# A quantised 3x3 convolution and a 7x7 involution: six x buffers instead of five, and narrower band buffers

## The chip, the cores and the metric

The kernel runs on one core of one Trainium2 chip. The metric is the device time of one execution in microseconds (us). Three runs of the kernel before were taken; a profile of one further execution gives every view quoted below.

## The reference, cut to what matters

```python
# x: (32, 256, 32, 32) float32
# layer 0
x = x + quant_conv3x3(group_norm(x), weight, bias)      # 256 -> 256 channels, values rounded to fp16's range and mantissa
# layer 1, an involution: every pixel has its own 7x7 kernel, one for each of 16 groups of channels
g = group_norm(x)
y = relu(bn(w1 @ g))                                    # 256 -> 64 channels
w = w2 @ y + b2                                         # 16 groups * 49 taps, for every pixel
x = x + sum over the 49 taps k of w[group, k, pixel] * g[channel, pixel + offset(k)]
```

`group_norm` has 32 groups of 8 channels; it needs the sums over a whole image before it can scale one element, so that an image passes through the kernel in stages.

## The kernel before, in words

An image is two halves of 128 channels by 1024 pixels, 1 MB of float32. One loop over steps `n` runs everything; an image takes `per` = 16 steps, and each piece of work on image b stands at a fixed distance from step 16 b. The order of the work on every engine is written out by this loop; nothing is rearranged later.

- **Loading x.** `load_x` (line 106) issues two transfers of 512 KB on SyncE's queue (SP), at step 16 b - 63, some four images ahead. The tile comes from the pool `xpool` with 5 buffers (line 94): the tile of image b takes the room of image b - 5.
- **The front** (`front`, from step 16 b - 56) is group norm, the 3x3 convolution on TensorE (line 332, `pc`), the residual addition, the second group norm, `py` (line 377) and the transposition of the normalised pixels (line 396, `pt`).
- **The involution's weights.** `weights` (line 411, eight calls for an image) makes the 49 x 16 weights of four rows of pixels; VectorE moves them into the ring `w_sb` (line 435). `scatter` (line 476, SP's queue) writes them to DRAM (`wd`) in the layout of a band matrix, 7 transfers of 160 KB for each of the 4 blocks k of eight rows of an image.
- **The bands.** `load_bands` (line 497) reads a block back from `wd` into one of three band buffers, by 16 transfers of 40 to 70 KB: 14 on GpSimd's queue (POOL), 2 on SP's (`BY_SYNC`). A band buffer has two sides, left and right half of the rows of pixels, each with `WINC` = 22 columns of `WB` = 160 floats and a pad of 8 floats.
- **The sums.** `sums` (line 522) multiplies bands and pixels on TensorE, two calls for a block (one for each side), eight for an image; of the 22 columns of a side it reads 19 (`WINI`), since three lie outside of the image. `add_windows` (line 538, VectorE) adds the result to x in place.
- **The stores.** `store` (line 543, SP's queue) writes half an image, 512 KB, when its sums are added. The second store of image b - 5 stands two steps before the load of image b, and the load writes the same buffer.

SP's queue is in order. Around the load of x it has, for every image: ... the last scatters, the second store, two band loads (block 2), **the two loads of x**, four scatters (block 0 of the next image), two band loads (block 3), three and four scatters (blocks 0 and 1), two band loads, and so on. In the compiled program the first of the two loads of x waits for the landing of the second store. Also, SP's transfers take eight semaphores in turn, so that each issue waits for the landing of the transfer eight places before it, where it doesn't wait for more. Counted so, the fourth scatter after the loads of x takes the semaphore of that store.

Of the kernel before, what the change touches and what calls it, by code (L numbers as in the profile page):

```python
# [9 lines left out]
F32 = mybir.dt.float32  # L10
# [3 lines left out]
P = 128  # L14
# [6 lines left out]
K1, PAD1 = 7, 3  # L21
# [15 lines left out]
XR = 4  # L37
# [3 lines left out]
SIDES = 2  # L41
JC = W // SIDES
K = H // TR
M = K * SIDES
WIN = XR + K1 - 1
WINC = JC + K1 - 1
WINI = JC + PAD1


# [2 lines left out]
V = 2  # L52
A = G // V
WB = G * WIN
PAD = V * (TR - XR)
WPIX = K1 * WB + PAD
SW = K1 * G
S = H + 2 * PAD1
T = 4
# [2 lines left out]
PAIRS = G // 2  # L62
ROW = S * WPIX
WR = 4
NBAND = 3
# [5 lines left out]
EARLY = CH + 4 + CH * CR  # L71
LATE = K1 * SW + 2 * 2 * SW
FRONT = -56
# [5 lines left out]
def tile_quant_conv_then_involution(  # L79
# [11 lines left out]
    PSUM = bass.MemoryType.PSUM  # L91

    const = ctx.enter_context(tc.tile_pool(name="const", bufs=1))
    xpool = ctx.enter_context(tc.tile_pool(name="xpool", bufs=5))
    small = ctx.enter_context(tc.tile_pool(name="small", bufs=2))
    work = ctx.enter_context(tc.tile_pool(name="work", bufs=2))
    dram = ctx.enter_context(tc.tile_pool(name="dram", bufs=1, space=bass.MemoryType.DRAM))
# [41 lines left out]
        nc.gpsimd.memset(t, 0.0)  # L139

    y_sb = [const.tile([P, N // 2], F32, name=f"y_{i}") for i in range(2)]
    bands = [const.tile([P, SIDES, WINC * WB + PAD], F32, name=f"band_{i}") for i in range(NBAND)]
    for t in bands[CH:]:
        nc.gpsimd.memset(t, 0.0)
    pixels = [const.tile([P, 2, PAIRS, PAIR], F32, name=f"pixels_{i}") for i in range(NPIX)]
# [4 lines left out]
    w_sb = const.tile([P, 2, RING, A, WIN, V], F32, name="w_sb")  # L150
    wd = dram.tile([H, S, WPIX], F32, name="wd")
    acc = [ps_acc.tile([P, RG, NT], F32, name=f"acc_{d}") for d in range(SIDES)]
# [14 lines left out]
    nc.sync.dma_start(late_sb, late)  # L167
    w2_sb = late_sb[:, : K1 * SW].rearrange("p (k n) -> p k n", n=SW)
    b2_sb = late_sb[:, K1 * SW :].rearrange("p (e r n) -> p e r n", r=2, n=SW)

# [10 lines left out]
    for col, cols, at, n in (  # L181
# [4 lines left out]
        to = bass.AP(  # L186
            tensor=wd.tensor,
            offset=wd.offset + col * WPIX + at,
            ap=[[ROW, H], [WPIX, cols], [1, n]],
        )  # L190
# [212 lines left out]
    def weights(b, r0):  # L403

        pws = [ps_w.tile([P, 2, 2, SW], F32, tag=f"pw{i}", name=f"pw{i}") for i in range(2)]
        for r in range(2):
# [58 lines left out]
    def scatter(b, k, part):  # L465

        at = (b * H + k * TR) % RING
        for dj in range(part, K1, 2):
            t, e = divmod(dj, 2)
            to = bass.AP(  # L470
                tensor=wd.tensor,
                offset=wd.offset + k * TR * ROW + dj * WPIX + (K1 - 1 - dj) * WB,
                ap=[[WPIX, TW], [ROW, TR], [1, WB]],
            )
# [3 lines left out]
    def load_bands(b, k):  # L478

        band = bands[(b * K + k) % NBAND]  # L480
        side = WINC * WB + PAD
        for i, j in enumerate(ORDER):
            cut = max(0, PAD1 - j)
            n = (K1 - cut) * WB + PAD
            src = bass.AP(
                tensor=wd.tensor,
                offset=wd.offset + k * TR * ROW + (j + PAD1) * WPIX + cut * WB,
                ap=[[ROW - V, TR], [(W - 1 - 2 * j) * WPIX - cut * WB, SIDES], [1, n]],
            )
            to = band[j::JC]  # L490
            to = bass.AP(
                tensor=to.tensor,
                offset=to.offset + (j + cut) * WB,
                ap=[to.ap[0], [side + (JC - 1 - 2 * j - cut) * WB, SIDES], [1, n]],
            )
            queue = nc.sync if j in BY_SYNC else nc.gpsimd
            queue.dma_start(to, src)  # L497

    def windows(b, m):


        k, d = divmod(m, SIDES)
        for g in range(RG):
            top = k * TR + g * XR - PAD1
            at = acc[d][:, g, : CH * WINI * WIN].rearrange("p (h j r) -> p h j r", h=CH, r=WIN)
            yield g, at, top, max(top, 0), min(top + WIN, H)

    def sums(b, m):

        k, d = divmod(m, SIDES)  # L510
        j0 = 0 if d else PAD1
        band = bands[(b * K + k) % NBAND][:, d]
        px = pixels[(b * K + k) % NPIX][:, d]
        for h in range(CH):
            for v in range(2):
                for g, at, top, f, l in windows(b, m):
                    p = slice(g * KP, (g + 1) * KP)
                    of = band[p, V * g * XR + j0 * WB : V * g * XR + (j0 + WINI) * WB]
                    of = of.rearrange("p (j a r v) -> p j a r v", a=A, r=WIN, v=V)
                    for t in range(T):  # L520
                        a = h * T + t
                        nc.tensor.matmul(  # L522
                            at[t * TW : (t + 1) * TW, h, :, f - top : l - top],
                            px[p, a, v * GC : v * GC + TW],
                            of[:, :, a, f - top : l - top, v],
                            start=(h, v) == (0, 0),
                            stop=(h, v) == (CH - 1, 1),
                        )
# [20 lines left out]
    def due(n, lag):  # L549

        b, i = divmod(n - lag, per)
        return (b, i) if 0 <= b < B else (None, None)

    with tc.manual_schedule():
        fronts = {}
        for n in range(FRONT, B * per + 2):
            b, i = due(n, FRONT)
# [12 lines left out]
            b, i = due(n, 0)  # L570
            if b is not None and i % 2 == 0:
                sums(b, i // 2)
            b, i = due(n, 1)
# [6 lines left out]
            b, i = due(n, 2)  # L580
            if b is not None and i == 2 * (M - 1 - SIDES):
                store(b, 0)
            b, i = due(n, -LEAD)
# [3 lines left out]
            for part in range(2):  # L587
                b, i = due(n, -LEAD + 1 + part)
# [4 lines left out]
            b, i = due(n, LOAD)  # L593
# [3 lines left out]
            b, i = due(n, 3 - 4 * NBAND)  # L597
            if b is not None and i % 4 == 0:
                load_bands(b, i // 4)
# [38 lines left out]
```

## Time and profile before

| | us |
|---|---|
| median of three runs | 1356.12 |
| lowest and highest | 1348.22 and 1360.93 |
| the profiled execution | 1344.24 |
| its span, first to last instruction | 1342.5 |
| TensorE busy in the span | 1253.6 (93%) |
| GpSimd (POOL) busy | 1014.4 (76%) |
| VectorE (DVE) busy | 818.8 (61%) |
| ScalarE (ACT) busy | 733.3 (55%) |

The profile names an instruction by its line, engine, operation and tiles, as `out<-in`. "A <- B" in a list of waits means that A's engine stood idle until B was done. "issue" is idle time for which no awaited event is found. PE is TensorE, SPq the queue of SyncE, where each item is the issue of a transfer. The DMA share in tables of time windows is the mean busy share of the core's 16 DMA engines (where it is over 1, packets overlap).

### The profile page before, as it was taken

How to read it: one execution, taken by the hardware profiler on the slowest of the kernel's cores; microseconds unless marked ns; L12 is line 12 of the kernel's file. 1: busy time of each engine (PE TensorE's matmuls, PEld its weight loads, DVE VectorE, ACT ScalarE, POOL GpSimd, SP SyncE). 2: the span in 40 equal slices, each digit the busy share in tenths (PEclk: the TensorE clock that was granted, in tenths of full speed). 3: DMA queues.
4: the chain of work that ended last, by engine and by line, in shares of the span. 5: the costliest groups of instructions: out<-in, count | busy, mean ns of one | idle time of the engine just before them, and what ended most of it. 6: DMA issues, size and time to landing. Idle time of an engine off the chain costs nothing.

```text
span 1342.5 us, 65799 instructions
## 1 busy us (share of the span) xinstructions
PE 1253.6 (93%) x27648; PEld 763.7 (57%) x27648; DVE 818.8 (61%) x2539; ACT 733.3 (55%) x1731; POOL 1014.4 (76%) x1818
## 2 busy tenths in 40 slices
PE   5899999999999999999999999999999999999665
PEld 2356566565555655556655556666555566556454
DVE  3466666565666665656665666766666666666442
ACT  5775656455656556556545655655556564553300
POOL 9067878777787778777778787788777877788785
PEclk9999999999999999999999999999999999999987
DMA  6089999999999999999999999999999999999995
GB/s 228 11 237 295 271 293 293 279 266 281 272 286 282 291 285 270 283 263 280 293 282 283 270 288 282 293 297 296 281 288 275 277 284 290 271 281 266 278 274 166
DMA packets 360724, 361.85 MB, mean 270 GB/s; under 512 B 75056, under 2 KB 304752, under 8 KB 359152
## 3 DMA queue, kind: packets, MB, share of 16 engines
q1 hardware_dynamic: 278512, 229.38, 56.8%
q0 software_dynamic: 81920, 128.28, 33.9%
q8 instruction: 220, 3.60, 1.1%
q14 instruction: 72, 0.59, 0.1%
HBM read 176.60 MB, written 180.76 MB: 266 GB/s over the span
## 4 chain that ended last, share of the span: by engine, by line
PE 60%; DMA 23%; POOL 7%; issue 3%; ACT 3%; DVE 2%; SPq 1%; POOLq 0%; DVEq 0%; ACTq 0%
PE pc L332 25%; PE acc L522 19%; DMA band<-wd 17%; PE pw L411 11%; POOL band L497 7%; DMA wd<-w_sb 6%; PE pt L396 3%; PE py L377 3%; ACT junk L214 1%; SPq L476 1%; DVE w_sb L435 1%; DMA x<-in_x 1%; ACT xn L273 0%; SPq L497 0%; ACT xq L273 0%
## 5 line engine op out<-in xcount | busy, mean ns | idle before, releaser
L497 POOL DMA_DIRECT2D band<-wd x1792 | 980.3, 549 | 315.7 <-DMA band<-wd 182.0
L435 DVE TENSOR_TENSOR w_sb<-pw,late_sb 128x224 f32<-128x224 f32 (+7 forms) x1280 | 330.4, 322 | 419.5 <-PE pw L411 419.2
L332 PE MATMUL pc<-xq,wq 128*128 128x496 f16 (+3 forms) x2304 | 535.2, 379 | 20.3 <-ACT xq L273 18.3
L522 PE MATMUL acc<-band,pixels 64*32 64x190 f32 (+1 forms) x16384 | 426.6, 332 | 51.8 <-DMA band<-wd 42.7
L522 PEld LDWEIGHTS acc<-band,pixels 64*32 64x32 f32 x16384 | 304.7, 107 | 159.7 <-issue 81.1
L332 PEld LDWEIGHTS <-wq 128*128 128x128 f16 x2304 | 206.7, 98 | 316.1 <-issue 102.7
L411 PE MATMUL pw<-late_sb,y 64*32 64x224 f32 (+1 forms) x8192 | 288.9, 333 | 10.8 <-issue 9.4
L538 DVE TENSOR_TENSOR x<-acc,x 128x380 f32<-128x380 f32 (+1 forms) x512 | 262.0, 512 | 32.2 <-PE acc L522 23.2
L411 PEld LDWEIGHTS pw<-late_sb,y 64*32 64x32 f32 x8192 | 186.5, 106 | 38.1 <-issue 21.0
L400 ACT COPY pixels<-pt 128x512 f32<-128x512 f32 x128 | 73.7, 576 | 228.6 <-PE pt L396 228.6
L214 ACT ACTIVATE junk<-x 128x512 f16<-128x512 f32 (+1 forms) x192 | 146.4, 763 | 14.7 <-DVE x L348 12.2
L214 ACT ACTIVATE junk<-x,mean 128x1024 f16<-128x1024 f32 x128 | 147.1, 1149 | 4.3
L245 ACT ACTIVATE s<-back,eps 128x2 f32<-128x2 f32 x64 | 18.9, 296 | 178.6 <-DVE back L230 178.6
L346 DVE TENSOR_SCALAR q<-pc 128x512 f16<-128x512 f32 x128 | 87.2, 681 | 17.6 <-PE pc L332 17.6
L273 ACT ACTIVATE xn<-x,off,rstd 128x512 f32<-128x512 f32 x128 | 96.2, 800 | 0.0
L348 DVE SCALAR_TENSOR_TENSOR x<-q,early_sb,x 128x512 f32<-128x512 f16 x128 | 94.2, 736 | 0.3
L396 PEld LDWEIGHTS pt<-ident,xn 128*128 128x128 f32 x512 | 63.9, 142 | 26.3 <-issue 2.5
L396 PE MATMUL pt<-ident,xn 128*128 128x128 f32 x512 | 78.0, 275 | 0.1
L273 ACT ACTIVATE xq<-x,off,rstd 128x1024 f16<-128x1024 f32 x64 | 75.7, 1227 | 0.0
L235 ACT ACTIVATE mean<-back 128x2 f32<-128x2 f32 x64 | 12.6, 196 | 101.4 <-DVE back L230 101.4
L377 PE MATMUL py<-xn,early_sb 128*64 128x512 f32 x256 | 62.2, 606 | 0.9 <-ACT xn L273 0.9
L224 DVE STREAM_TRANSPOSE across<-sums 128x32 f32<-128x32 f32 x128 | 26.3, 205 | 33.6 <-ACT junk L214 32.4
(40 smaller groups left out, 369.3 us busy)
## 6 DMA issues: line engine op xcount, KB each, us to landing
wd<-w_sb SPq DMA_DIRECT2D x896, 160.0 KB
band<-wd POOLq DMA_DIRECT2D x1664, 70.5 KB, 4.6
x<-in_x SPq DMA_DIRECT2D x64, 512.0 KB
out<-x SPq DMA_DIRECT2D x64, 512.0 KB
band<-wd POOLq DMA_DIRECT2D x128, 60.5 KB, 4.6
band<-wd SPq DMA_DIRECT2D x128, 50.5 KB
band<-wd SPq DMA_DIRECT2D x128, 40.5 KB
band<-in_w SPq DMA_DIRECT2D x2, 1152.0 KB
```

The lines of the kernel that those rows point to most:

```text
L214: nc.scalar.activation(junk[:, n0:n1], src[:, h, n0:n1], func, bias=bias, accum_out=self.sums[:, i : i + 1])
L273: nc.scalar.activation(dst, src, AF.Identity, bias=self.off[:, one], scale=self.rstd[:, one])
L332: nc.tensor.matmul(pc.rearrange("p (r c) -> p r c", c=W)[:, r0 - nt * RT : r1 - nt * RT, c0:c1], wq[:, kh, k, mh * P : (mh + 1) * P], xq[: ...
L346: nc.vector.tensor_scalar(q, pc, F16_MAX, -F16_MAX, ALU.min, ALU.max)
L348: nc.vector.scalar_tensor_tensor(xt[:, mh, cols], q, bias_sb[:, mh : mh + 1], xt[:, mh, cols], ALU.add, ALU.add)
L377: nc.tensor.matmul(py[i * CR : (i + 1) * CR], w1_sb[:, kh, :], px[:, :, i], start=kh == 0, stop=kh == CH - 1,)
L396: nc.tensor.transpose(pt[:, i, h * P : (h + 1) * P], xn[:, h, (m + i) * P : (m + i + 1) * P], ident)
L411: nc.tensor.matmul(pws[i][t * TW : (t + 1) * TW, : dj.stop - dj.start, r], y_sb[b % 2][half, (r0 // 2 + r) * W : (r0 // 2 + r + 1) * W], w ...
L435: nc.vector.tensor_tensor(to, of[:, :, d0:d1], bias[:, :, d0:d1], ALU.add)
L497: queue.dma_start(to, src)
L522: nc.tensor.matmul(at[t * TW : (t + 1) * TW, h, :, f - top : l - top], px[p, a, v * GC : v * GC + TW], of[:, :, a, f - top : l - top, v], ...
L538: nc.vector.tensor_tensor(x_at, of, x_at, ALU.add)
```

## The change

`xpool` gets six buffers, so that the tile of image b takes the room of image b - 6. To make room, a side of a band buffer keeps only the 19 columns that are inside the image: its length `SIDE` is `WINI * WB + PAD` = 3048 floats in place of 3528. The left side drops its first three columns, the right side its last three; the destination offsets in `load_bands` and the operand's offset in `sums` follow. No transfer and no matmul changes its size or its number. Three memsets of a band buffer cover 6096 elements a partition in place of 7056.

```diff
-WINC = JC + K1 - 1
 WINI = JC + PAD1
...
 WPIX = K1 * WB + PAD
+SIDE = WINI * WB + PAD
...
-    xpool = ctx.enter_context(tc.tile_pool(name="xpool", bufs=5))
+    xpool = ctx.enter_context(tc.tile_pool(name="xpool", bufs=6))
...
-    bands = [const.tile([P, SIDES, WINC * WB + PAD], F32, name=f"band_{i}") for i in range(NBAND)]
+    bands = [const.tile([P, SIDES, SIDE], F32, name=f"band_{i}") for i in range(NBAND)]
...
     def load_bands(b, k):
 
         band = bands[(b * K + k) % NBAND]
-        side = WINC * WB + PAD
...
-                offset=to.offset + (j + cut) * WB,
-                ap=[to.ap[0], [side + (JC - 1 - 2 * j - cut) * WB, SIDES], [1, n]],
+                offset=to.offset + (j + cut - PAD1) * WB,
+                ap=[to.ap[0], [SIDE + (JC - 1 - 2 * j - cut + PAD1) * WB, SIDES], [1, n]],
...
     def sums(b, m):
 
         k, d = divmod(m, SIDES)
-        j0 = 0 if d else PAD1
...
-                    of = band[p, V * g * XR + j0 * WB : V * g * XR + (j0 + WINI) * WB]
+                    of = band[p, V * g * XR : V * g * XR + WINI * WB]
```

In the compiled program every engine's instructions keep their order. The first of the two loads of x, from image 5 on, loses its wait for the store; the fourth scatter behind it gains one for the same store.

## The prediction

> **What bounds the kernel now.** I read the page first, then the time by windows, the waits of TensorE and of the queues, and last the timeline of SP and POOL around one load of x. The page has TensorE busy for 93% of the span and 9 in nearly all slices of its DMA row, so two resources are close to full. The windows say how close. The first two lines are stretches of 200 us in the steady part, the other three are three images with no gap on TensorE at all:
>
> ```profile
> 340.00:540.00 200.00, 194.12 (x4393) 118.66 (x4400) 127.89 (x399) 115.22 (x274) 152.66 (x280) 1.00 0.97 282
> 940.00:1140.00 200.00, 193.86 (x4364) 117.67 (x4348) 126.76 (x395) 114.63 (x273) 153.88 (x283) 1.00 0.97 282
> ...
> 795.06:833.00 37.94, 37.94 (x865) 23.41 (x865) 25.26 (x80) 22.75 (x55) 29.21 (x54) 1.00 0.98 290
> 833.00:871.05 38.05, 38.05 (x865) 23.21 (x864) 25.28 (x80) 22.78 (x55) 29.65 (x55) 1.00 0.97 285
> 871.05:908.99 37.94, 37.94 (x865) 23.17 (x864) 25.26 (x80) 22.75 (x55) 30.49 (x56) 1.00 0.98 295
> ```
>
> The first number is the length, the second TensorE's busy time, the last two the DMA share and GB/s. An image costs TensorE 37.9 to 38.05 us when nothing stops it. The mean period is longer: the 27 loads of x that wait start between 136.2 and 1166.7 us, so 1030.5 / 26 = 39.6 us. So about 1.6 us of each image could go, 43 us over 27 images, before TensorE alone is the bound. The DMA engines stand at 0.96 to 0.98 in both kinds of stretches.
>
> What TensorE lacks, and what the queues wait for:
>
> ```profile
> PE acc L522 <- DMA band<-wd: 29.3, 18, 4.6
> ...
> POOL band L497 <- DMA band<-wd: 153.7, 193, 2.9
> POOL band L497 <- DMA wd<-w_sb: 21.6, 22, 3.1
> ...
> SPq L476 <- DVE w_sb L435: 73.5, 51, 5.1
> SPq L106 <- DMA out<-x: 69.4, 25, 4.1
> SPq L476 <- DMA x<-in_x: 14.4, 18, 1.6
> ```
>
> (total us, times, longest; TensorE's line between 80 and 1300 us, the others between 140 and 1140.) TensorE's largest wait with a named cause is for bands. POOL, which issues most of them, waits for their landings (153.7 us) and for scatters (21.6), hardly ever for a band buffer. So the stream evict, scatter, band load is late, and the DMA engines set its pace. SP stands 69.4 us in front of the loads of x, 2.8 us an image, until the store of the buffer's last owner has landed.
>
> One load of x on SP:
>
> ```profile
> 610.41 0.58 SPq L543 DMA_DIRECT2D out<-x  x1
> 611.09 2.17 SPq L497 DMA_DIRECT2D band<-wd  x2
> 616.29 1.57 SPq L106 DMA_DIRECT2D x<-in_x  x2
> 618.54 2.54 SPq L476 DMA_DIRECT2D wd<-w_sb  x4
> ```
>
> SP is free at 613.26 and issues at 616.29. The DMA engines during such holes (four us each, from 2 us before a load of x to 2 us after):
>
> ```profile
> 614.29:618.29 4.00, 4.00 (x107) 2.74 (x106) 2.71 (x10) 3.11 (x6) 3.66 (x7) 1.00 0.74 179
> 693.04:697.04 4.00, 4.00 (x107) 2.74 (x105) 2.98 (x10) 2.29 (x4) 3.29 (x7) 1.00 0.72 201
> 773.54:777.54 4.00, 4.00 (x103) 2.91 (x106) 3.18 (x11) 2.08 (x4) 3.35 (x7) 1.00 0.79 204
> 851.62:855.62 4.00, 4.00 (x107) 2.74 (x106) 2.65 (x10) 2.74 (x6) 3.26 (x7) 1.00 0.83 213
> 889.85:893.85 4.00, 4.00 (x107) 2.71 (x106) 2.67 (x10) 3.00 (x6) 3.20 (x7) 1.00 0.84 218
> 965.66:969.66 4.00, 2.75 (x73) 2.09 (x78) 2.49 (x9) 2.77 (x6) 2.58 (x6) 1.00 0.89 250
> ```
>
> The reader is to see the share fall to 0.72 to 0.89, and at first without harm: TensorE is full in five of the six.
>
> [...] all SP issues behind the load of x stand still until 616.29. [...] in this image POOL waits 0.93 and 1.14 us for band landings at 621.5 and 623.0, while x drains. [...]
>
> **The change part by part.**
> 1. The wait at line 106 goes: 77.1 us in 27 waits over the whole span, 2.86 us each. SP can issue x at once (613.3 in the image shown). Behind it, three scatters need only evictions and older landings; the evictions of the right `weights` call (TensorE 611.85 to 612.9 us) are done at about 614. The fourth scatter now waits for the store, which landed at about 616.2, and was issued at about 620.2 before. So scatters of block 0 move up by 2 to 4 us, and so do the landings of x that the next scatters wait for (14.4 us, 18 times). None of this is time by itself: SP waits 73.5 us for evictions elsewhere in the steady part, 2.9 us an image, so its lead is taken back there.
> 2. The hole is filled. The mean of the six shares above is 0.80; with 0.89, 0.77 and 0.93 measured for three more loads it is 0.82. Against the 0.965 of the steady part this is 0.143 x 4 us = 0.57 us of all DMA engines for an image; against 1.00, 0.71 us. If the DMA engines set the pace, this comes off the period: 27 x 0.57 = 15.4 us, at most 27 x 0.71 = 19 us. Nothing, if another latency takes over. I take 15.4.
> 3. POOL's waits for scatters (21.6 us in the steady part) lie in about half of the cases 13 to 16 us after a load of x, at block 0 of the next image (1.90 us at 630.88 in the image shown). They shrink. I book no further gain for it: POOL's transfers behind are paced by the engines that item 2 already counts.
> 4. Narrower bands: a memset of 5.97 us covers 6096 in place of 7056 elements, 5.16 us, so 0.81 us less three times. The first frees SP's zero writes 0.8 us sooner; TensorE starts at 15.24 us behind ScalarE, and the first band load stands at 71.7 us. Zero; at most 0.8 us. Matmuls and transfers have the same shapes; their offsets differ, and I take nothing for it.
> 5. The first 136 us and the end after 1167 us have no load of x that waits; the end, where TensorE waits 2 to 4.6 us at a time for bands, stays.
>
> Sum: 1344.24 - 15.4 = 1328.8 us for the profiled execution (span 1342.5 and 1.7 around it). The median of the three runs is 11.9 us above this execution, so I subtract the same from 1356.12: **1340.7 us**, 1.1% faster.
>
> **Rivals.**
> - *The gain is lost (1351 us, 0 to 8 us off).* The hole costs little, because POOL's loads use it: they get more of the engines then. Filled, the hole only moves the slowness from the band loads after it to those within it. For: TensorE is full in five of six holes, and three images in a row ran at 38 us with holes in them. Against: bytes that move earlier can't be in the way later. At 0.2 us an image, 5 us.
> - *Slower (1372 us).* One mechanism: the x load now collides with the POOL loads of block 2, which run just then (608.78 to 618.45 us in the image shown). Block 2's last landing, 617.90 plus the median 4.6 us, is 622.5, and TensorE wants it at 624.72, so there are 2.2 us to spare. From first to last issue blocks that meet x now (block 3) take 9.9 us in the mean, block 0, without x, 8.0; if these 1.9 us move to block 2 and no lead is won, the slack is gone in half of the images, at some 1.2 us each: 27 x 0.6 = 16 us. It decides once block 2 slips by over 2.2 us. Against: the POOL stream as a whole gets no more work.
> - *More (1321 us).* SP's lead of 2 to 4 us keeps scatters ahead in all blocks, and most images reach 38.3 us: 27 x 1.3 = 35 us. Against: the waits for evictions in item 1.
> - *It doesn't do what it says:* the load could be stopped by another semaphore. Its own two semaphores belong to scatters eight places back, which have landed by then in the image shown; 3% within "lost".
>
> **How the numbers follow.** Chances: forecast 0.43 (8 to 21 us off), lost 0.30, slower 0.12, more 0.15. A measurement of this kernel tells about 1%, 13.6 us, from no change. Over 1% faster: all of "more" and 0.30 of the forecast, 0.45; within 1%: the rest of the forecast, "lost", and part of the slower case's weak form (0.02 of it), so 0.45; slower by over 1%: 0.10. The range reaches to "more" and to a half-sized slower case: 1322 to 1364.
>
> **What would show it.** Right: no SP wait for `out<-x` at the load of x; a DMA share around it of 0.95 or more; period of the loads 39.0 us; POOL's waits for scatters below 12 us; TensorE's waits for bands fewer. Wrong: the share stays at 0.8 (another wait took its place); or share filled and period still 39.6 (lost); or TensorE waiting at block 2, 7 to 12 us after x, in most images (slower).

## The result, and the profile after

The changed kernel takes 1366.85 us (median of 13 runs, 1360.91 to 1375.31); the kernel before takes 1354.56 us in 13 runs beside it. The ratio is 1.0103, with a 95% interval of 1.0072 to 1.0134: slower by 1.0%, where 1.1% faster was forecast; the range given ended at 1364 us. The profiled execution has a span of 1370.5 us. Executions of either kernel differ by some 10 us to both sides; a second profile of the changed kernel (below, "again") has a span of 1346.3 us and the same pattern of waits. So the ratios of many runs carry the verdicts here, and of the profiles only what returns in several. Runs more than 1.5% above their kernel's fastest are left out of the ratios (one of narrow5's and one of rev1k's below are among them).

Item 1 of the prediction's working came true, and item 2's first half too. In the changed kernel's file `load_bands` is line 496, `sums` 520 and `store` 541. First windows of the steady part, then the stretches around and behind one load of x (length, TensorE busy, other engines, granted clock, DMA share, GB/s):

```profile
140.00:1140.00 1000.00, 952.82 (x21282) 578.81 (x21279) 625.88 (x1954) 564.80 (x1340) 755.98 (x1382) 1.00 0.96 277
340.00:540.00 200.00, 190.26 (x4294) 116.02 (x4276) 124.36 (x387) 113.19 (x269) 151.67 (x278) 1.00 0.96 275
940.00:1140.00 200.00, 190.12 (x4222) 114.53 (x4219) 125.67 (x394) 112.74 (x269) 149.85 (x274) 1.00 0.96 277
```

```profile
576.60:580.60 4.00, 4.00 (x89) 2.50 (x69) 2.16 (x9) 0.77 (x3) 3.73 (x8) 1.00 1.11 320
580.60:590.60 10.00, 7.80 (x208) 5.16 (x208) 4.87 (x15) 4.57 (x11) 5.45 (x11) 1.00 0.95 279
590.60:600.60 10.00, 9.83 (x216) 6.10 (x215) 6.58 (x18) 7.52 (x18) 7.31 (x14) 1.00 0.92 261
```

The second fence follows one load of x at 578.60 us. The hole is gone: 1.11 in the four microseconds in which the kernel before had 0.72 to 0.89. Over the 26 loads between 140 and 1190 us the mean is 1.04 (309 GB/s), where the kernel before has 0.85 (236 GB/s). But in the ten microseconds behind this load TensorE loses 2.2 us, and in the next ten the share is 0.92. The hole was not removed, it moved. These are the means of GB/s over the images between 140 and 1150 us, counted from the issue of the second store, some 3 us before the changed kernel's load and 6 us before the old one's:

| | 4 to 8 us | 16 to 20 us | 24 to 28 us |
|---|---|---|---|
| before | 236 | 274 | 249 |
| after | 270 | 225 | 229 |
| again | 270 | 242 | 231 |

The share over the whole steady part doesn't tell the kernels apart: it is 0.97 before and 0.96 after, but 0.97 in again and 0.96 in narrow5 and pause6, two kernels below that keep the time of the kernel before.

The queue's timeline around this load, and SP's waits between 140 and 1140 us:

```profile
575.26 0.98 SPq L541 DMA_DIRECT2D out<-x  x1
576.34 2.16 SPq L496 DMA_DIRECT2D band<-wd  x2
578.60 1.00 SPq L106 DMA_DIRECT2D x<-in_x  x2
579.96 3.54 SPq L476 DMA_DIRECT2D wd<-w_sb  x4
583.61 1.86 SPq L496 DMA_DIRECT2D band<-wd  x2
586.94 7.07 SPq L476 DMA_DIRECT2D wd<-w_sb  x7
```

```profile
SPq L476 <- DVE w_sb L435: 146.2, 76, 8.3
SPq L476 <- DMA x<-in_x: 59.9, 43, 3.7
SPq L476 <- DMA wd<-w_sb: 23.2, 34, 2.0
```

The load goes out 0.1 us after the band loads, and no wait for `out<-x` is left in front of it. Its 69.4 us have gone to two other places in the same queue: scatters wait 45.5 us more for the landing of x (59.9 for 14.4), since they now reach the shared semaphores early, and 72.7 us more for evictions (146.2 for 73.5; in again 62.6 and 129.1). SP gained no lead that anybody could use.

Where TensorE's time went: its waits between 80 and 1200 us in the changed kernel (total us, times, longest),

```profile
PE pw L411 <- issue: 17.9, 14, 3.4
PE acc L520 <- issue: 12.9, 13, 2.4
PE acc L520 <- DMA band<-wd: 7.4, 8, 1.9
PE acc L520 <- DMA x<-in_x: 4.2, 3, 2.4
PE pc L332 <- issue: 4.2, 2, 3.9
...
PE pt L396 <- issue: 0.9, 1, 0.9
```

and in the kernel before:

```profile
PE acc L522 <- DMA band<-wd: 14.9, 12, 2.7
PE pw L411 <- issue: 8.5, 14, 1.1
PE acc L522 <- issue: 3.6, 5, 1.2
...
PE pc L332 <- issue: 0.4, 1, 0.4
```

The waits for bands halve, as the prediction wished (14.9 to 7.4). The waits called "issue", for which the profile has no awaited event, grow from 12.5 to 35.9 us. This is nearly all that the two executions differ by: from the 1,501st to the 24,301st of TensorE's matmuls the changed kernel takes 1073.2 us and the kernel before 1048.5, 24.7 of the 28.0 us between their spans, and the issue waits are 23.4 us of it. One of them, in TensorE's timeline 10 us after the load of x:

```profile
584.82 0.60 PE L396 MATMUL pt<-ident,xn 128*128 128x128 f32 x4
585.35 0.88 PE L520 MATMUL acc<-band,pixels 64*32 64x190 f32 x23
588.43 1.07 PE L520 MATMUL acc<-band,pixels 64*32 64x190 f32 x36 [2.20 <-issue]
```

TensorE stops in the middle of the 64 matmuls of one call of `sums`, and the profile has no semaphore there that it waits for. What goes with such stops stands in the DMA part of the page:

```profile
q8 instruction: 220, 3.60, 1.1%
```

These are 220 packets of 16 KB in the queue "instruction". The trace has 56,456 instructions of TensorE (55,296 matmuls and weight loads, and 1,160 others), 256.6 for a packet; 220 x 256 is 56,320. Two things tie the packets to the "issue" stalls of TensorE over 0.5 us after 80 us, of which the changed kernel has 22 and the kernel before 14. First, in all 36 the last such packet had ended 1.2 to 1.7 us before TensorE went on. Second, counted through all of TensorE's instructions in the trace, all 36 stalls stand at the same two neighbouring places of a period of 256. Over the 17 profiles of this document the first holds for 271 of 277 stalls and the second for 272; a place that had nothing to do with the period would fall on these two once in 128. So I read these stalls as TensorE out of instructions, with a packet bringing the next 256; no line of the profile says this outright. In the case above the packet began at 585.7 and ended at 587.0, and the packet before it had begun 10.1 us before this one, where 1370.5 / 220, some 6 us, is the mean; over the 22 stalls it had begun 8.0 us before in the mean. The packets themselves take hardly longer than in the kernel before (mean 1.09 us for 1.08); it is their start that is late. Most of the 220 packets go with no such stall, but 22 do, and single stalls reach 3.9 us. TensorE goes through 256 instructions in only 39.6 x 256 / 1760, some 5.8 us (an estimate from the period and 56,320 / 32 instructions an image).

### The profile page after: what moved, and what is told of

Its sections match the earlier page's. It is cut to its first block, busy times and chain, and to the rows that moved or that the text cites. A ratio compares the mean times of both kernels' runs of the same rounds, so it can differ in the third digit from the quotient of the medians.

```text
span 1370.5 us, 65798 instructions
## 1 busy us (share of the span) xinstructions
PE 1254.9 (92%) x27648; PEld 764.4 (56%) x27648; DVE 823.7 (60%) x2539; ACT 733.3 (54%) x1731; POOL 1010.8 (74%) x1818
## 4 chain that ended last, share of the span: by engine, by line
PE 66%; DMA 17%; issue 5%; POOL 4%; ACT 4%; DVE 3%; SPq 1%; POOLq 0%; ACTq 0%
PE pc L332 27%; PE acc L520 21%; PE pw L411 12%; DMA band<-wd 10%; POOL band L496 4%; DMA wd<-w_sb 3%; PE py L377 3%; PE pt L396 3%; DMA x<-in_x 2%; ACT junk L214 1%; DVE w_sb L435 1%; SPq L496 1%; ACT xn L273 1%; DMA band<-in_w 1%; DVE wq L195 1%
## 5 line engine op out<-in xcount | busy, mean ns | idle before, releaser
L411 PE MATMUL pw<-late_sb,y 64*32 64x224 f32 (+1 forms) x8192 | 286.2, 331 | 19.3 <-issue 17.9
L245 ACT ACTIVATE s<-back,eps 128x2 f32<-128x2 f32 x64 | 18.9, 296 | 185.7 <-DVE back L230 185.7
```

Source lines behind the costliest of these rows:

```text
L411: nc.tensor.matmul(pws[i][t * TW : (t + 1) * TW, : dj.stop - dj.start, r], y_sb[b % 2][half, (r0 // 2 + r) * W : (r0 // 2 + r + 1) * W], w ...
```

## The experiments

Theory after the result: the early megabyte of x joins the second store and the band loads without a gap in front of it, and the DMA engines are then late with TensorE's instruction packets. Rivals: the new layout of the bands costs; the load costs whatever its place; long runs in the load block the others; what stands behind x in SP's queue is late. "Issue" stands below for TensorE's issue stalls between 80 and 1200 us, summed from each kernel's list of waits. It belongs to one execution, the profiled one, whose time stands beside it; the ratio comes from all runs of a kernel and those of the kernel before beside it.

| kernel | runs | ratio to the kernel before | 95% interval | profiled, us | issue, us |
|---|---|---|---|---|---|
| before | | 1 | | 1344.24 | 12.5 |
| after | 13 | 1.0103 | 1.0072 to 1.0134 | 1372.24 | 35.9 |
| again: after once more | 20 | 1.0081 | 1.0059 to 1.0103 | 1348.03 | 25.9 |
| narrow5 | 22 | 0.9993 | 0.9972 to 1.0013 | 1347.21 | 21.8 |
| pause6 | 14 | 1.0014 | 0.9984 to 1.0045 | 1354.43 | 22.4 |
| early74 | 7 | 1.0053 | 1.0018 to 1.0088 | 1363.67 | 28.8 |
| pause74 | 12 | 0.9998 | 0.9968 to 1.0029 | 1352.96 | 17.2 |
| late60 | 4 | 1.0147 | 1.0111 to 1.0184 | 1363.83 | 40.8 |
| rev1k | 4 | 1.0114 | 1.0056 to 1.0172 | 1346.27 | 21.7 |
| actq | 7 | 1.0088 | 1.0050 to 1.0125 | 1356.70 | 18.7 |
| burst8 | 20 | 1.0010 | 0.9990 to 1.0030 | 1353.51 | 19.3 |
| spread4 | 4 | 0.9868 | 0.9826 to 0.9909 | 1326.03 | 11.1 |
| spread8 | 4 | 0.9856 | 0.9802 to 0.9911 | 1321.18 | 8.8 |
| stores4 | 4 | 0.9845 | 0.9786 to 0.9904 | 1330.57 | 10.2 |
| rows8 | 4 | 0.9898 | 0.9858 to 0.9937 | 1330.79 | 6.9 |
| five8 | 4 | 1.0225 | 1.0169 to 1.0281 | 1368.13 | 3.8 |
| eighth | 4 | 0.9674 | 0.9641 to 0.9707 | 1310.62 | 6.1 |

**Buffer or layout.** narrow5 undoes the buffer alone:

```diff
-    xpool = ctx.enter_context(tc.tile_pool(name="xpool", bufs=6))
+    xpool = ctx.enter_context(tc.tile_pool(name="xpool", bufs=5))
```

> The narrow band buffers of the change with five buffers for x: the load of x waits for the store again. If the sixth buffer is what costs (theory: the early megabyte of x makes the DMA engines late for TensorE's instructions and for the bands), the time is that of the kernel before, ratio 0.995 to 1.005, SP waits some 2.8 us for out<-x at each load of x, and TensorE's waits with the cause 'issue' stay near 13 us. If the new layout of the bands costs (rival), the ratio is about 1.01 as with the whole change.

The ratio is 0.9993: the narrow bands cost and bring nothing, the sixth buffer is the whole loss. The issue stalls came out at 21.8 us, not near 13, so that this sum varies by some 10 us from execution to execution.

again runs the changed kernel a second time.

> The changed kernel once more, for a second profile beside the other kernels: ratio 1.007 to 1.014; issue stalls of TensorE between 80 and 1200 us at 25 to 40 us where the kernel before has 12.5; no SP wait for out<-x in front of the load of x.

It repeats the loss (1.0081), and the stalls (25.9 us) are again above those of the kernel before. Its profiled execution is 7.4 us faster than the median of its runs, 1355.44 us, so that its stalls are those of a fast execution.

**The place of the load.** late60 has `LOAD = -60` and early74 `LOAD = -74` in the changed kernel, both without a wait.

> The change with the load of x three steps later in SP's order, behind the seven scatters of block 0, still without a wait. If the collision of x with what is on the DMA engines just then is the cause (theory), moving x away from the second store and block 2's loads and behind the scatters brings the ratio to the kernel before to 0.99 to 1.00, and fewer 'issue' stalls of TensorE. If it is the sixth buffer itself, or SP running ahead without a brake (rival), the ratio stays at 1.01.

> The change with the load of x eleven steps earlier, behind the scatters of block 0 one image earlier, in a stretch of SP's order with no store near it; six buffers allow it. Theory (the place of the megabyte decides): ratio 0.98 to 1.00, and TensorE's stalls move with the load, to some 8 to 12 us after its new place, if they stay. Rival (a load without a wait costs wherever it stands): ratio about 1.01.

late60 contradicts its theory: later in SP's order is no better, and beside again's 1.0081 worse, 1.0147. early74, 1.0053, is not below 1 either, and can't be told from again. But the stalls follow the load. In the changed kernel 24 of 30 issue stalls lie at the third and fourth of an image's eight calls of `sums` and the work behind them; in late60 20 of 39 and in early74 19 of 26 at the fifth and sixth. late60's list is nearly nothing but such stalls:

```profile
PE pw L411 <- issue: 23.6, 22, 2.6
PE acc L520 <- issue: 16.0, 15, 2.6
...
PE acc L520 <- DMA band<-wd: 0.6, 2, 0.3
```

**The bytes.** eighth loads 128 columns of x in place of 1024 from image 6 on, into six fixed tiles; the rest of a tile keeps older values, so that it prices the bytes and leaves out most of the input.

```diff
...
+        cols = N if b < 6 else N // 8
         for h in range(CH):
-            nc.sync.dma_start(xt[:, h], x[b, h * P : (h + 1) * P])
+            nc.sync.dma_start(xt[:, h, :cols], x[b, h * P : (h + 1) * P, :cols])
```

> The change with an eighth of each x loaded from image 6 on (1/8 of the columns, 128 KB in place of 1 MB; the rest of the tile keeps older values); six fixed tiles. It prices the bytes. Theory: TensorE's 'issue' stalls some 8 to 12 us after the load come from the x bytes ahead of the instruction packets, so they fall from about 30 us to under 8 us, and the time falls by 40 us or more, to 1310 to 1330 us (ratio 0.97 to 0.98). Rival (the stalls come from the phase of the program, not from the bytes): they stay above 20 us though the time falls.

```profile
PE pw L414 <- issue: 4.1, 4, 1.9
PE acc L523 <- issue: 1.8, 5, 0.5
...
PE pt L399 <- issue: 0.2, 1, 0.2
```

The stalls fall from 26 to 36 us to 6.1 us, with the same instructions on TensorE: it is the bytes of x that the stalls come from. Against the changed kernel's 1.008 to 1.010, a ratio of 0.9674 is 4.1 to 4.3%, some 55 to 58 us for all that these bytes cause.

**Lump or runs.** spread8 and spread4 cut a load into pieces of 256 and 512 columns and spread them over the steps that the sixth buffer allows; burst8 has the eight pieces at one place. `LOADS` is -77, -75, ..., -63 in spread8, -76, -72, -68, -64 in spread4 and eight times -63 in burst8.

```diff
-            b, i = due(n, LOAD)
-            if i == 0 and b > 1:
-                x_tiles[b] = load_x(b)
+            for p in range(PIECES):
+                b, i = due(n, LOADS[p])
+                if i == 0 and b > 1:
+                    load_x(b, [p])
```

> The change with each x loaded in eight pieces of 128 KB (256 columns of one half), one every second step over the 16 steps before the image is needed. The megabyte as one lump is what holds up the packets that bring TensorE's instructions (theory), so the stalls of TensorE with the cause 'issue' fall from about 30 us to under 12 us and the ratio to the kernel before is 0.980 to 0.995. If the bytes cost the same wherever they lie (rival), the stalls are spread out but not fewer, and the ratio is 1.00 to 1.01.

> The change with each x in four pieces of 256 KB, one every four steps. Theory (the lump): between the eight pieces and the whole, ratio 0.985 to 1.000, issue stalls 12 to 20 us. Rival (the bytes cost the same anywhere): 1.00 to 1.01.

> The change with the same eight pieces of 128 KB, all at the place of the change's load, one behind the other: runs of 1 KB a partition in place of 4 KB, and eight issues for two. Theory (the lump in time counts): ratio 1.01 as with the change, or a little above, since six more issues and semaphores lie in SP's queue. Rival[...]: ratio 1.00 or less, and issue stalls under 20 us.

Spread, the megabyte costs much less: 0.9856 and 0.9868. SP waits only 5.8 us in front of pieces of x here (69.4 before, both between 140 and 1140 us), so that its running ahead is not the loss by itself. The steady part of spread8, which beats both kernels, and its TensorE waits between 80 and 1200 us:

```profile
140.00:1140.00 1000.00, 985.87 (x22212) 601.70 (x22197) 651.41 (x2033) 587.83 (x1393) 789.43 (x1444) 1.00 1.00 288
```

```profile
PE acc L527 <- DMA band<-wd: 4.5, 7, 1.2
PE acc L527 <- issue: 3.5, 7, 0.9
PE pw L418 <- issue: 3.2, 8, 0.7
PE pc L339 <- issue: 2.1, 3, 0.9
```

The moved hole is gone as well: in the three stretches after the second store (4 to 8, 16 to 20, 24 to 28 us) the mean is 281, 280 and 280 GB/s.

burst8 was a surprise: 1.0010 at the place where two loads give 1.0103 or 1.0081. The pieces have runs of 1 KB where the loads have 4 KB, so two kernels took the runs apart from the number of pieces: rev1k keeps two loads at the same place with runs of 1 KB, rows8 spreads eight pieces with runs of 4 KB.

```diff
+        def chunks(at, n=256):
+            step, size = at.ap[-1]
+            return bass.AP(
+                tensor=at.tensor, offset=at.offset + size - n, ap=[at.ap[0], [-n, size // n], [1, n]]
+            )
...
+            to, of = xt[:, h], x[b, h * P : (h + 1) * P]
...
+                nc.sync.dma_start(chunks(to), chunks(of))
```

`chunks` (rev1k, from image 2 on) takes the quarters of a row in reverse order.

> The change with its two loads of x at their place, from image 2 on cut into runs of 1 KB (the four quarters of a row in reverse order[...]); number of issues, semaphores and waits are those of the change. If the runs of 4 KB are what holds up instruction packets and bands, as the eight pieces at one place suggest (ratio 1.001), the ratio is 0.995 to 1.004 and the issue stalls between 80 and 1200 us fall from 36 to about 20 us. If it was the six further issues and their waits that slowed SP down in that run (rival), the ratio stays at 1.007 to 1.013.

> Eight pieces of 128 KB spread over 16 steps at the places of the spread of eight, but cut by partitions: 32 partitions with whole runs of 4 KB each. If the lump in time is what counts, ratio 0.982 to 0.992 as with the spread by columns. If the length of the runs counts (rival), the spread by rows keeps most of the loss: 0.995 to 1.01.

Long runs in spread pieces keep most of the gain (0.9898), so spreading helps with either length. That short runs in two loads leave the loss (1.0114) is shown less firmly: the three runs behind it took 1346.27, 1354.51 and 1360.06 us beside a median of 1345.17 us, which is 1.007 by the plain medians. Together they speak for the lump in time and against the length of its runs. The expectation of fewer stalls with short runs can't be read from rev1k's 21.7 us: its profiled execution is the one of 1346.27 us, which shows next to none of the loss. What sets burst8 apart is how its pieces go out: they take SP 5.1 us where the changed kernel's two loads take 1.0,

```profile
572.78 5.10 SPq L113 DMA_DIRECT2D x<-in_x  x8
```

and that is not SP's own pace alone. The eight pieces take all eight semaphores, so that the later ones wait for the store and the band loads in front of them: between 80 and 1200 us SP waits 5.7 us for `out<-x` and 10.8 us for `band<-wd` in front of pieces of x, 27 times. So burst8 spreads the lump over five microseconds and has a part of the old pause back. Which of the two makes its 1.0010 was not tested.

**What SP's wait did.** pause6 keeps six buffers and puts a transfer of 4 bytes in front of the load, which has to wait for the second store of image b - 5; pause74 does the same at early74's place with a read of the last scatter's bytes.

```diff
+        if b - 5 in stored:     # pause6; stored[b] is the tile of image b after its last store
+            nc.sync.dma_start(stored.pop(b - 5)[:1, 0, N - 1 :], x[b, :1, N - 1 :])
         for h in range(CH):
             nc.sync.dma_start(xt[:, h], x[b, h * P : (h + 1) * P])
```

> The change, six buffers, with one transfer of 4 bytes in front of the two loads of x that must wait for the landing of the previous image's second store (it overwrites one element of the tile that was just stored). SP's pause of the kernel before is back, the buffer isn't. If the pause is what the change lost (theory), ratio 0.996 to 1.004 and issue stalls between 80 and 1200 us back at 12 to 23 us. If the place in the other buffer or anything else counts (rival), ratio 1.006 to 1.012.

> The load of x eleven steps earlier (ratio 1.005 without a pause), with a read of 4 bytes in front of it that must wait for the last scatter in front to land. If a drained queue in front of the megabyte is what helps at any place (theory), ratio 0.990 to 1.001 and fewer issue stalls than the 28.8 us of the same place without the pause. Rival (the pause helps only behind the store, where block 2's bands use it): 1.003 or more.

```profile
SPq L108 <- DMA out<-x: 85.4, 27, 4.4
```

With SP held up for 85.4 us again (between 80 and 1200 us), the time is back: 1.0014, with an interval below those of after and again. So it is the lost wait that made the changed kernel slower. At the other place the pause takes 1.0053 to 0.9998; those two intervals overlap, so it is likely rather than shown there. The wait that the change removed was doing work: SP issued nothing in it, and the megabyte met emptier DMA engines (203 GB/s in the mean of the four microseconds around pause6's 26 loads, for 309 in the changed kernel), and the stretches after the second store are those of the kernel before again (214, 287 and 255 GB/s). The pause holds back the scatters behind x as well as x; the two were not held back apart.

**Queue, buffers, stores.** actq issues x from ScalarE (`nc.scalar.dma_start`), five8 spreads eight pieces with five buffers (`LOADS` from -63 to -58), stores4 adds cut stores to spread8.

> The change with the loads of x issued by ScalarE at the same step[...], so that the scatters behind them in SP's queue don't stand behind the megabyte. If scatters and bands standing behind x in one queue cost (rival), ratio 0.995 or less. If the DMA engines' load is what delays instruction packets (theory), the issue stalls stay at 20 to 35 us, and the ratio is 1.005 to 1.015.

> The eight pieces by columns with five buffers for x: the first still waits for the store, and all eight must lie in six steps, since the buffer comes free only then. If the sixth buffer is worth something only because it lets the load be spread, this lies between the kernel before and the spread of eight: ratio 0.990 to 1.002. If cutting alone does it, 0.985 to 0.990, and the sixth buffer isn't needed.

> The spread of eight, with each store of 512 KB cut into its two halves of channels, the second half one or two steps later. If lumps cost wherever they come from (theory), a little faster than the spread of eight: ratio to the kernel before 0.978 to 0.986. If only the load of x matters (rival), 0.986 to 0.990.

actq keeps the loss (1.0088), so standing behind x in SP's queue is not the cause; its issue stalls are fewer than expected, 18.7 us, and TensorE's waits for bands more, 18.1 us, so that the loss looks different there. five8 came out far above both expectations, 1.0225: with five buffers the pieces can only lie in the last six steps, and the last ones are late (waits between 140 and 1140 us):

```profile
ACT junk L221 <- DMA x<-in_x: 87.3, 34, 5.5
...
PE py L384 <- ACT xn L280: 40.4, 31, 2.3
```

Its issue stalls are the lowest of all, 3.8 us, but it also stops TensorE for 40.4 us in other places (that instructions catch up there is a guess and not shown); ScalarE waits 87.3 us for x. With five buffers this spread doesn't pay, with six it does. stores4, 0.9845, can't be told from spread8.

## Why the prediction was wrong

1. *The wait goes (item 1).* Right: none is left. Right also that it is no time by itself; the waits for evictions rose by 72.7 us.
2. *The hole is filled, and 15.4 us come off (item 2).* This is the step that failed. The hole was filled (share 1.11 where 0.72 to 0.89 was), but what was filled there did not come off the period: "if the DMA engines set the pace" took it that the hole was spare time and that nothing else would be late for it. A hole of the same kind opened some 12 us later (225 GB/s for 274, 16 to 20 us after the store). The page counts the instruction packets in the time of the same 16 engines (220 packets, 1.1%). Filling the hole put a megabyte straight behind a store and band loads, and instruction packets came late (8.0 us behind the one before in the mean of the 22 stalls, where some 6 us is the mean of all): TensorE's issue stalls went from 12.5 to 35.9 us (25.9 in again), a term that the sum put at nothing. What was booked as 15.4 us gained was about 12 us lost (1366.85 - 1354.56). The hole was also a little smaller than booked: 0.85 over 26 loads, where the nine in the prediction had 0.82.
3. *POOL's waits for scatters shrink (item 3).* They didn't: 21.6 us before, and after

```profile
POOL band L496 <- DMA band<-wd: 165.7, 203, 2.8
...
POOL band L496 <- DMA wd<-w_sb: 21.6, 21, 2.9
```

4. *The bands (item 4).* Right to cost nothing, by narrow5.
5. *The ends (item 5).* Up to TensorE's 1,501st matmul the changed kernel's profile is 1.4 us behind, and from the 24,301st on it takes 2.0 us more; the ends were not tested apart.

Of the rivals, "slower" had the sign and the collision, and with 16 us for the 12 measured nearly the size, but that is luck, since it had another mechanism. Block 2's loads do take longer from first to last issue (10.6 us in the mean between 80 and 1200 us, 8.9 before) and block 3's shorter (9.2 for 10.0), yet TensorE's waits for bands fell from 14.9 to 7.4 us, and most stalls lie at the calls for block 1, before block 2 is wanted. Of "the gain is lost" the traces show the premise: from 2 us before to 2 us after the load POOL's queue moved 128 GB/s in the old kernel (mean of the 26 loads between 140 and 1190 us) and 94 in the changed one, where the steady part has 101 and 99. The prediction's argument against it, that bytes that move earlier can't be in the way later, is what the runs refute. The rival that should have been on the list stood in the same list of TensorE's waits from which I quoted only the largest: three lines "issue", 16.0 us between 80 and 1300 us. I left a wait without a named cause unread. Between the first two profiles the issue stalls account for the difference; that they make up the whole of the lasting loss of 11 to 14 us is not shown. Over the profiles with a pause (before, narrow5, pause6) they average 18.9 us, over those without (after, again, rev1k) 27.8 us, 9 us more; but the sums vary by 10 us between executions of like kernels, single ones of the two groups meet at 22 us, and two of the latter three executions, again's and rev1k's, are faster than their kernel's median. What delays the start of an instruction packet is not shown; the runs show that the stalls follow the bytes of x (eighth, 6.1 us) and their density in time (spread8, 8.8 us).

## What to carry to other kernels

A wait that a queue makes in front of a large load may be what keeps the load apart from the burst before it (1.0103 without it, 1.0014 with it again); before removing it, ask what the transfer will meet when it starts early. A spare buffer is worth more as room to spread a load (0.9856) than as leave to start it at once (1.0103). And stalls that the profile calls "issue" in the middle of released work belong next to the times of the instruction packets: at a DMA share of 0.96 the changed kernel has 35.9 us of them, and all 22 over 0.5 us ended 1.2 to 1.7 us after such a packet.

## What the runs showed of the hardware

The page lists 220 packets of 16 KB in a queue "instruction" and counts them in the time of the 16 DMA engines (1.1%); that is one for 256.6 of TensorE's 56,456 instructions. In 36 of 36 stalls over 0.5 us, in two profiles, TensorE went on 1.2 to 1.7 us after such a packet had ended, and in 272 of 277, in 17 profiles, it stopped at the same two neighbouring places of a period of 256 of its instructions; single stalls reached 3.9 us. A DMA share near 1 did no harm by itself: spread8 has 1.00 in its steady part, with 8.8 us of such stalls, and the changed kernel has 0.96 and 0.97 with 36 and 26 us. Behind two of the changed kernel's stalls, of 2.4 and 3.9 us, TensorE's granted clock was 0.5 for 3.41 us, behind four others of 2.0 to 3.4 us it was not. The kernel before has two such stretches between 80 and 1200 us too, behind waits for bands of 2.2 and 2.7 us, and spread8 has none.
